# A second buffer for the turned sums of a softmax, and one instead of two for their quarters

## The chip, the cores and the metric

The kernel runs on one core of a Trainium2 chip. The metric is the device time of one execution in microseconds (us), the median of several runs. The profile is of one such execution. The engines are called as the profile has them: PE is the tensor engine (matrix products, into PSUM), DVE is VectorE, ACT is ScalarE, and SP issues the transfers (DMAs).

## What is computed

Two layers of the same kind, one after the other, on `x` of shape (4, 128, 96, 96) in float32. A layer is a block of attention over the pixels of an image, cut here to its lines:

```
g     = maxpool2(conv1x1(x, g_w, g_b))          # 64 channels, 48*48 = 2304 keys
phi   = maxpool2(conv1x1(x, phi_w, phi_b))      # 64 channels, 2304 keys
theta = conv1x1(x, theta_w, theta_b)            # 64 channels, 96*96 = 9216 queries
attn  = softmax(theta^T phi)                    # over the 2304 keys
y     = attn g
x     = W_w y + W_b, normalised by bn_*, + x
```

The divisor of the softmax, one sum of 2304 exponentials for each query, is what the change is about.

## The kernel before

**Tiling.** Keys lie on partitions, queries along the free dimension. The 2304 keys are 18 tiles of 128. The 9216 queries are nine *pairs* of 2 x 512. For one pair and one tile of keys, `scores` (L347) lets PE make a 128 x 1024 tile of products and ACT take its exponential (L357) into one of seven `exp` buffers; `add_up` (L360) lets DVE add that tile to the pair's running `sum` (L366; the first time L364); `values` (L368) lets PE multiply it by `gT` into `av` (L374). After the last tile ACT copies `av` to `halves` (L381): two partial results of 512 columns, which `add_halves` (L453) adds.

**Steps and cycles.** The order of the work on each engine is written out by hand. There are 8 blocks (four images, two layers) of nine pairs, and nine steps of two key tiles to a pair: 648 steps. In step `t`, PE makes the scores of step `t` and then the values of step `t - 1`. Eighteen steps are a *cycle*: its even pair takes s = 0 to 8, its odd pair s = 9 to 17. What else there is to do stands at fixed places s of the cycle:

```
TURNS, HALVES, INVERT = (8, 4), (12, 2), (13, 6)
NORM, PROJECT = (1, 10), (3, 12)
```

The first number is for the even pair, the second for the odd one. A number smaller than the pair's own steps means a place in the next cycle, where the two pairs of the cycle before are called `gone`. So the even pair is turned at s = 8 and 9, inverted at 13, normalised at 1 of the next cycle and projected at 3; the odd pair is turned at 4 and 5 of the next cycle, inverted at 6, normalised at 10 and projected at 12. In the last cycle the even pair's halves and invert come at s = 10 already.

**The divisor.** `sum` has, for each query, 128 partial sums, one on each partition. `turn(h)` (L415) transposes one half of it, 128 x 512, in squares of 32 x 32 into `turned` (L422), and reduces that to 16 columns of `parts` (L423). After both halves, `invert` (L428) transposes the four quarters of `parts` into `four` (L433), reduces them to one sum for each query (L434), takes the reciprocal (L437) and notes the sums for a later check (L438). The reciprocals must then be spread: every query's to all 64 channels. For that two DMAs write them as two rows of 512 into `turned`, whose contents are no longer needed (L443), and two more broadcast each row to 64 partitions of `halves` (L448), which is `rc`. `normalise` (L457) multiplies by it (L458); `multiply` (L460) is the projection on PE (L464), into the two PSUM banks of the tag `misc`; `add` (L469) is DVE's reading of them (L473), with the shift and the residual, back into `x`.

**What else uses the two `misc` banks.** The keys and values of the next block are made in chunks beside the current one, with products on PE (L208, `gphi_ps`) and pooling on DVE (L234). They start at s = 13, 15 and 17 while there are chunks left to make. The next pairs' `theta` (also L208) is made at s = 5.

**Buffers and queues.** The pool `work` has two buffers for a tag where nothing else is said. `turned` has one; `parts`, `sum`, `halves`, `four` and `both` have two. [...] The broadcasts and the stores of the results are issued from the queue of SP.

Of the kernel before, what the change touches and what calls it, by code (L numbers as in the profile page):

```python
# [9 lines left out]
F32 = mybir.dt.float32  # L10
# [6 lines left out]
P = 128  # L17
# [3 lines left out]
QT = 512  # L21
# [22 lines left out]
SQ = 32  # L44
# [9 lines left out]
def shifted_blocks(ctx: ExitStack, tc: tile.TileContext, x: bass.AP, layers, out: bass.AP, flag):  # L54
# [30 lines left out]
    work = ctx.enter_context(tc.tile_pool(name="work", bufs=2))  # L85
# [222 lines left out]
    class Pair:  # L308
# [106 lines left out]
        def turn(self, h):  # L415

            if h == 0:
                self.turned = work.tile(
                    [P, QT], F32, tag="turned", name=f"turned_{self.name}", bufs=1
                )  # L420
                self.parts = work.tile([P, SQ], F32, tag="parts", name=f"parts_{self.name}")
            nc.vector.transpose(self.turned, self.sum[:, ts(h, QT)])  # L422
            nc.vector.tensor_reduce(  # L423
                self.parts[:, ts(h, QT // SQ)],
                self.turned.rearrange("p (b k) -> p b k", k=SQ), AX.X, ALU.add,
            )

        def invert(self):  # L428

            four = work.tile([SQ, P // SQ, SQ], F32, tag="four", name=f"four_{self.name}")  # L430
            both = work.tile([SQ, 2, SQ], F32, tag="both", name=f"both_{self.name}")
            for k in range(P // SQ):
                nc.vector.transpose(four[:, k, :], self.parts[ts(k, SQ), :])  # L433
            nc.vector.tensor_reduce(  # L434
                both[:, 0, :], four.rearrange("p k q -> p q k"), AX.X, ALU.add
            )
            nc.vector.reciprocal(both[:, 1, :], both[:, 0, :])  # L437
            nc.vector.tensor_reduce(notes[:SQ, self.number, :], both, AX.X, ALU.add)  # L438
            self.rc = self.halves[:, QT:]
            n = QT // SQ  # L440
            for h in range(2):
                row = self.turned[h * CI : h * CI + 1, :]
                nc.sync.dma_start(  # L443
                    out=row.rearrange("o (b k) -> o b k", k=SQ), in_=both[ts(h, n), 1, :]
                )
            for h in range(2):
                row = self.turned[h * CI : h * CI + 1, :]
                nc.sync.dma_start(  # L448
                    out=self.rc[ts(h, CI), :],
                    in_=row.unsqueeze(1).to_broadcast([1, CI, QT]),  # L450
                )
# [565 lines left out]
```

## Time and profile before

| what | before |
|---|---|
| median of three runs | 2587.36 us (2585.7 to 2587.54) |
| span of the profiled execution | 2584.3 us |
| DVE: transposes into `turned` (L422) | 142, 705 ns each |
| DVE: reduction of `turned` (L423) | 142, 686 ns each |
| DVE: transposes into `four` (L433) | 284, 199 ns each |
| SP: DMAs of reciprocals into rows of `turned` (L443) | 142, 2 KB each |
| SP: broadcasts from `turned` into `halves` (L448) | 142, 128 KB each |

A group of the profile has its line, engine and operation, its operands as out<-in with their shapes, then how often it ran, and busy time and mean duration. A list of waits has who waited (engine, tile, line), for whom, and then us in all, times and the longest. A timeline has start and length in us; neighbours of one kind are merged, with their number after the x; the bracket at the end has the idle time of the engine before the instruction and what ended it. A matmul's end is modelled and matmuls overlap, so the start of the next one tells more than the length of one. A product of float32 takes two matmul instructions here: one step's scores, two tiles of four products, are 16 of them.

### The profile page before, as it was taken

To read this page: it belongs to the slowest core of one execution; us is meant where nothing else is said; L and a number is where in the kernel's file an instruction comes from. 1 tells how busy PE (TensorE), PEld (TensorE's weight loads), DVE (VectorE), ACT (ScalarE), POOL (GpSimd) and SP (SyncE) were. 2 spreads that over 40 slices of the span, in tenths; PEclk is the share of its full clock that TensorE was granted. 3 is DMA by queue.
4 is the path that set the end of the run, shared out by engine and by line. 5 is a ranking of instruction groups with operands and counts; after the bars stand their busy time and mean duration, and the time that the engine had idled before them with its cause. 6 is when DMAs were issued, how large, how long until landed. Compare 5 with 4: busy or idle time off the path is not lost.

```text
span 2584.3 us, 53389 instructions
## 1 busy us (share of the span) xinstructions
PE 2512.7 (97%) x23058; PEld 1119.8 (43%) x23058; DVE 2122.9 (82%) x2684; ACT 1542.0 (60%) x1511; POOL 0.7 (0%) x6
## 2 busy tenths in 40 slices
PE   9999999999999999999999999999999999999998
PEld 4344434444354443444433444344443354433332
DVE  7888888888888888888888888888888888888887
ACT  5555655556655566555666556555566565666664
POOL 0000000000000000000000000000000000000000
PEclk9999999999999999999999999999999999999999
DMA  4113111111121122222112212211111221122222
GB/s 151 9 6 83 10 10 9 7 8 10 9 18 22 25 26 18 18 18 70 10 10 17 26 22 26 25 10 9 9 7 9 21 23 23 24 26 26 26 26 35
DMA packets 26888, 60.43 MB, mean 23 GB/s; under 512 B 8330, under 2 KB 9236, under 8 KB 26644
## 3 DMA queue, kind: packets, MB, share of 16 engines
q1 hardware_dynamic: 26476, 56.88, 19.5%
q8 instruction: 182, 2.98, 0.5%
q14 instruction: 62, 0.51, 0.1%
q10 hardware_dynamic: 168, 0.07, 0.0%
HBM read 19.14 MB, written 18.87 MB: 15 GB/s over the span
## 4 chain that ended last, share of the span: by engine, by line


## 5 line engine op out<-in xcount | busy, mean ns | idle before, releaser
L357 ACT ACTIVATE exp<-sc,nshift 128x1024 f32<-128x1024 f32 x1296 | 1385.5, 1113 | 959.4 <-PE sc L351 957.9
L366 DVE TENSOR_TENSOR sum<-sum,exp 128x1024 f32<-128x1024 f32 x1151 | 1406.6, 1222 | 204.4 <-ACT exp L357 153.1
L351 PE MATMUL sc<-theta,phi 64*64 64x512 f32 x10368 | 1456.8, 589 | 0.8 <-ACT exp L357 0.8
L374 PE MATMUL av<-exp,gT 64*64 64x512 f32 x10368 | 1400.6, 590 | 0.0
L351 PEld LDWEIGHTS sc<-theta,phi 64*64 64x64 f32 x10368 | 531.5, 133 | 614.3 <-issue 523.0
L374 PEld LDWEIGHTS av<-exp,gT 64*64 64x64 f32 x10368 | 519.4, 133 | 611.0 <-issue 507.0
L422 DVE STREAM_TRANSPOSE turned<-sum 128x512 f32<-128x512 f32 x142 | 100.3, 706 | 174.2 <-DMA halves<-turned 174.2
L208 PE MATMUL gphi_ps<-x,gphiT 64*64 64x512 f32 x1056 | 202.5, 593 | 16.6 <-DVE x L473 16.6
L464 PE MATMUL W_ps<-halves,WT 64*64 64x512 f32 x568 | 84.2, 608 | 44.4 <-DVE halves L458 44.4
L234 DVE TENSOR_REDUCE gphi<-gphi_ps 128x128 f32<-128x512 f32 x144 | 92.3, 680 | 31.8 <-PE gphi_ps L208 24.8
L364 DVE TENSOR_TENSOR sum<-exp,exp 128x1024 f32<-128x1024 f32 x72 | 87.8, 1220 | 19.6 <-ACT exp L357 18.9
L381 ACT COPY halves<-av 128x1024 f32<-128x1024 f32 x71 | 71.9, 1012 | 50.2 <-PE av L374 50.2
L423 DVE TENSOR_REDUCE parts<-turned 128x16 f32<-128x512 f32 x142 | 97.4, 686 | 4.9
L473 DVE SCALAR_TENSOR_TENSOR x<-W_ps,shift,x 128x512 f32<-128x512 f32 x142 | 99.6, 743 | 0.0
L208 PEld LDWEIGHTS gphi_ps<-x,gphiT 64*64 64x64 f32 x1056 | 61.3, 132 | 86.7 <-DVE x L473 45.0
L208 PE MATMUL theta_ps<-x,thetaT 64*64 64x512 f32 x560 | 88.5, 589 | 0.0
L304 DVE STREAM_TRANSPOSE gT<-gphi 32x192 f32<-32x192 f32 x192 | 70.7, 368 | 3.5
L464 PEld LDWEIGHTS W_ps<-halves,WT 64*64 64x64 f32 x568 | 22.1, 133 | 93.3 <-DVE halves L458 75.3
L433 DVE STREAM_TRANSPOSE four<-parts 32x32 f32<-32x32 f32 x284 | 56.4, 199 | 2.9
L455 DVE TENSOR_TENSOR halves<-halves 128x512 f32<-128x512 f32 x71 | 48.5, 683 | 0.0
L458 DVE TENSOR_TENSOR halves<-halves 128x512 f32<-128x512 f32 x71 | 48.5, 683 | 0.0
L208 PEld LDWEIGHTS theta_ps<-x,thetaT 64*64 64x64 f32 x560 | 29.2, 133 | 34.6 <-issue 30.7
(75 smaller groups left out, 217.1 us busy)
## 6 DMA issues: line engine op xcount, KB each, us to landing
halves<-turned SPq DMA_DIRECT2D x142, 128.0 KB
out_dram<-x SPq DMA_DIRECT2D x35, 512.0 KB
x<-in_x_dram SPq DMA_DIRECT2D x18, 768.0 KB
x<-in_x_dram SPq DMA_DIRECT2D x12, 384.0 KB
turned<-both SPq DMA_DIRECT2D x142, 2.0 KB
out_dram<-x SPq DMA_DIRECT2D x4, 128.0 KB
gphi_nat<-in_L_conv_phi_w_dram SPq DMA_DIRECT2D x2, 32.0 KB
rows_other<-in_L_conv_g_b_dram SPq DMA_DIRECT2D x4, 0.2 KB
```

The source lines that it names most:

```text
L208: nc.tensor.matmul(out, lhsT=lhsT, rhs=rhs, start=step == 0, stop=step == 1)
L234: nc.vector.tensor_reduce(self.gphi[:, ts(k, KT)].rearrange("p (h w) -> p h w", w=w), ps.rearrange("p (h a w b) -> p h w a b", a=2, b=2, w=w),
L351: nc.tensor.matmul(ps[ts(c, CI), ts(h, QT)], lhsT=self.blk.phi[ts(h, CI), ts(2 * k + c, CI)], rhs=self.th[ts(h, CI), :], start=True, stop= ...
L357: nc.scalar.activation(e, ps, AF.Exp, bias=nshift)
L364: nc.vector.tensor_add(self.sum, self.es[0], e)
L366: nc.vector.tensor_add(self.sum, self.sum, e)
L374: nc.tensor.matmul(self.av[ts(h, CI), ts(r, QT)], lhsT=self.blk.gT[ts(r, CI), k, :], rhs=e[ts(r, CI), ts(h, QT)], start=(k == 0), stop=(k ...
L381: nc.scalar.copy(self.halves, self.av)
L422: nc.vector.transpose(self.turned, self.sum[:, ts(h, QT)])
L423: nc.vector.tensor_reduce(self.parts[:, ts(h, QT // SQ)], self.turned.rearrange("p (b k) -> p b k", k=SQ), AX.X, ALU.add,)
L464: nc.tensor.matmul(self.pss[h][ts(c, CI), :], lhsT=self.blk.w.W[ts(h, CI), ts(c, CI)], rhs=self.y[ts(h, CI), :], start=True, stop=True,)
L473: nc.vector.scalar_tensor_tensor(dst, self.pss[h], self.blk.w.shift, dst, op0=ALU.add, op1=ALU.add)
```

## The change

The tile `turned` gets two buffers, like the other tags of its pool. The rows in which a pair's reciprocals stand while they are spread are then not the ones that the next pair's sums are turned into. In turn `four` gets one buffer instead of two. In a partition's bytes `turned` takes 2048 more, and `four` 512 less.

```diff
             if h == 0:
                 self.turned = work.tile(
-                    [P, QT], F32, tag="turned", name=f"turned_{self.name}", bufs=1
+                    [P, QT], F32, tag="turned", name=f"turned_{self.name}"
                 )
                 self.parts = work.tile([P, SQ], F32, tag="parts", name=f"parts_{self.name}")
...
         def invert(self):
 
-            four = work.tile([SQ, P // SQ, SQ], F32, tag="four", name=f"four_{self.name}")
+            four = work.tile(
+                [SQ, P // SQ, SQ], F32, tag="four", name=f"four_{self.name}", bufs=1
+            )
             both = work.tile([SQ, 2, SQ], F32, tag="both", name=f"both_{self.name}")
```

Nothing else is changed.

## The prediction, made before the change was run

> **What bounds the kernel now.** The page comes first: which engine is full, and in every slice or only in some.
>
> ```profile
> PE 2512.7 (97%) x23058; PEld 1119.8 (43%) x23058; DVE 2122.9 (82%) x2684; ACT 1542.0 (60%) x1511; POOL 0.7 (0%) x6
> ```
>
> PE is the engine to relieve or to keep fed; VectorE at 82% and ScalarE at 60% have room. The page gives no chain (its part 4 is empty), so the path has to be found from the waits. The list of waits, cut to VectorE and to PE (us in all, times, longest us):
>
> ```profile
> DVE turned L422 <- DMA halves<-turned: 174.2, 35, 5.7
> PE W_ps L464 <- DVE halves L458: 44.4, 35, 5.3
> PE gphi_ps L208 <- DVE x L473: 16.6, 21, 0.8
> ```
>
> VectorE's longest wait is the one the change is aimed at: 35 times about 5 us. That alone is no gain, since VectorE has slack. The other two lines count: PE stands still for the projection (35 times, waiting for the normalise on L458) and for the next keys' chunk (21 times, waiting for the add on L473). 35 is also the number of cycles that have a previous odd pair. The timeline of VectorE in one cycle joins them (start us, length us, what; in brackets the idle time and its releaser):
>
> ```profile
> 1199.45 2.56 DVE L366 TENSOR_TENSOR sum<-sum,exp 128x1024 f32<-128x1024 f32 x2 [0.88 <-ACT exp L357]
> 1206.85 0.71 DVE L422 STREAM_TRANSPOSE turned<-sum 128x512 f32<-128x512 f32 x1 [4.85 <-DMA halves<-turned]
> ...
> 1213.13 0.68 DVE L458 TENSOR_TENSOR halves<-halves 128x512 f32<-128x512 f32 x1
> 1213.73 3.88 DVE L366 TENSOR_TENSOR sum<-sum,exp 128x1024 f32<-128x1024 f32 x3
> 1217.53 1.40 DVE L473 SCALAR_TENSOR_TENSOR x<-W_ps,shift,x 128x512 f32<-128x512 f32 x2
> ```
>
> The transpose of the even pair (s = 8) may not overwrite `turned` until the odd pair's broadcast out of its rows (issued at s = 6) has landed, at 1206.85. Everything VectorE has queued behind it is late, among it the normalise (s = 10) and the add (s = 12). Now PE in the same stretch:
>
> ```profile
> 1208.86 2.26 PE L374 MATMUL av<-exp,gT 64*64 64x512 f32 x16
> 1210.57 2.26 PE L351 MATMUL sc<-theta,phi 64*64 64x512 f32 x16
> 1213.87 1.09 PE L464 MATMUL W_ps<-halves,WT 64*64 64x512 f32 x8 [1.03 <-DVE halves L458]
> 1214.78 1.90 PE L374 MATMUL av<-exp,gT 64*64 64x512 f32 x16
> 1216.49 1.04 PE L351 MATMUL sc<-theta,phi 64*64 64x512 f32 x8
> 1218.33 1.31 PE L208 MATMUL gphi_ps<-x,gphiT 64*64 64x512 f32 x5 [0.79 <-DVE x L473]
> ```
>
> Read the starts, not the lengths. 16 matmuls take 1.72 us from start to start (1208.86 to 1210.57), so 8 take 0.86; a plain step of 32 takes 3.43 us and one with 8 more 4.29. Step 12 should be 4.29; from its first scores (1210.57) to the next step's (1216.49) it is 5.92, a loss of 1.63. The bracket says only 1.03, because a matmul counts as busy to its modelled end, past the point where its successor could have started. In step 13 the chunk was due 0.86 after 1216.49, at 1217.35, and started at 1218.33: 0.98 lost.
>
> I subtracted these nominal lengths from all 648 steps. Sixteen of the eighteen places in the cycle lose nothing or next to it (6.2 us in all at s = 1, where the values wait for ScalarE's copy of `av`). Step 12 loses 62.7 us in 35 cycles, 7.85 of them in the last; step 13 loses 21.5 us in 21 cycles. Why the last is so large:
>
> ```profile
> 2547.46 1.99 PE L464 MATMUL W_ps<-halves,WT 64*64 64x512 f32 x8 [5.31 <-DVE halves L458]
> 2549.22 3.34 PE L374 MATMUL av<-exp,gT 64*64 64x512 f32 x16
> 2552.39 1.89 PE L351 MATMUL sc<-theta,phi 64*64 64x512 f32 x16
> ```
>
> There the even pair's invert also stands ahead of the normalise at s = 10. PE idles 5.31 us, then needs 1.76 us for 8 matmuls and 3.17 for 16, twice the usual.
>
> [...] the idle times of about 1 us have no such sequel. [...] the sums of s = 9 and 10, whose exponentials were there, were done only after the transpose. [...] 97% hides 84 us, and the repeated hole of 4.85 us is a buffer's release.
>
> **The change, part by part.**
>
> *Second `turned`.* Pairs alternate, so even pairs have one buffer and odd pairs the other. The even transpose at s = 8 now needs the even pair's broadcast issued at s = 13 of the cycle before (thirteen steps, some 50 us earlier), and that pair's normalise, which waited for this landing, has run on VectorE at s = 1. The odd transpose at s = 4 likewise. The 174.2 us of waiting go. The landing is still needed by the odd pair's own normalise, so I place that again in the cycle shown, without the stall:
> - Transpose and reduce of the even pair from 1202.0 to 1203.4.
> - s = 9: its exponentials end near 1203.9; one sum (1.21) and the second turn (1.4), to 1206.4.
> - s = 10: its exponentials end at 1206.3 and 1207.4 (ScalarE starts them at 1205.22); two sums to 1208.8, the normalise to 1209.5.
> - The broadcast landed at 1206.85, 1.9 us before VectorE asks. PE wants the product at 1210.57 + 1.72 = 1212.28, 2.8 us after it is there. No wait is left.
>
> *The chunk at s = 13.* With no lag, the add at s = 12 is like that at s = 3, where no stall precedes: the scores start at 1177.10 and the adds run from 1180.85 to 1182.25, that is +3.75 to +5.15 us. The chunk is due at +4.29 + 0.86 = +5.15. Its first bank is free at +4.45, its second just in time. In the cycle shown the second bank was 1.58 us late against its due time and the loss was 0.98, so half a microsecond of lateness costs nothing. I take 0 and keep 0.1 us x 21 = 2 us for the range.
>
> *Last cycle.* From the transpose's start to the normalise's end are 2538.08 to 2547.40 = 9.3 us without a pause. Begun 5.65 earlier, the normalise ends at 2541.75; PE is due at 2540.25 + 1.72 = 2541.97. So it just fits, and the half clock is not entered: 7.85 us come back, or 7 if the margin of 0.2 is missed.
>
> *One `four`.* Its transposes overwrite what the reduce on L434 read nine steps and more earlier, on the same engine, whose order already gives that: nothing. The DMAs, their sizes and their order on the SP queue are the same. The normalise may need a wait of its own for the broadcast: the trace has 36 such events of 21 ns at L458 for the even pairs, so 35 x 0.02 = 0.7 us more on VectorE, in its slack.
>
> *Sum.* 62.7 + 21.5 = 84.2 us less, and some 1 us kept back for the chunk and the last cycle: 2587.36 - 83 = 2504.
>
> **The rivals.**
> - *Only the idle time of the page comes back*, or something is left of the wait at s = 12 and 13: 44.4 + 16.6 = 61.0, so 2526. For it: these are the only numbers that the profile calls waits. Against it: the starts of the matmuls, which show the steps longer by 84.
> - *The wait moves.* The normalise inherits the DMA wait and PE still waits: no change, 2587. It would take a landing 4.7 us later (1211.6 instead of 1206.85) before PE waits at all, and some 7 us later to lose what is lost now. The chain from the invert's end to the landing took 10.8 to 11.0 us in all 35 cycles.
> - *PE without its pauses is granted less clock*, slower: one half-rate window of 6.8 us (as at 2545) in each of 35 cycles would cost 3.4 x 35 = 119 us, 2504 + 119 = 2623. Against it: PE already runs some 60 us per cycle without a pause at full clock, and the only half-rate windows of the trace, apart from start and end, follow the idle time.
>
> **How the numbers follow.** Full gain 0.86, at 2504; part of it 0.08, at 2526; wait moves 0.03, at 2587; slower 0.03, at 2623. The predicted time is the first. A bottom of 2500 allows for 84 us, all of the hitches, and the spread of 1.8 us among the runs of before; the top of 2516 takes in 2 us at the chunk, 1 in the last cycle and 0.2 us left in each of 35 steps 12. Faster 0.94, same 0.03, slower 0.03.
>
> **What would show it.** Right: the wait of `turned` for the broadcast and both PE waits gone from the lists; VectorE's busy time the same at about 2123 us and its share up; step 12 at 4.29 us; the second sum before L422 and L422 itself back to back; no half clock before the end. Wrong: L458 with a DMA as its releaser, L208 still waiting for L473, PE starts wider than 0.86 us per 8 in plain steps, or more ScalarE or PE waits for exponentials' buffers.

## The result, and the profile after

| | before | after |
|---|---|---|
| median | 2586.82 us (2585.7 to 2587.54) | 2496.19 us (2495.89 to 2496.32) |
| span of the profiled execution | 2584.3 us | 2493.8 us |

The median of before is now of four runs, one more than ahead. The ratio is 0.965, with a 95% interval of 0.9633 to 0.9667: 90.6 us less, where 83 were forecast. The direction and the main mechanism held; the time lies 4 us below the range. In the changed kernel lines behind L430 are two higher: L458, L464 and L473 are now L460, L466 and L475.

The first part of the page after, busy time by engine:

```profile
PE 2483.7 (100%) x23058; PEld 897.7 (36%) x23058; DVE 2133.0 (86%) x2684; ACT 1541.7 (62%) x1511; POOL 0.7 (0%) x6
```

The same number of instructions on each engine as before, and PE has no pause left that the page can see. The list of waits after, for PE alone, is complete with four lines, all of them from the start or the end:

```profile
PE warm_ps L565 <- POOL ident masks.py:199: 1.4, 1, 1.4
PE sc L351 <- ACT exp L357: 0.8, 1, 0.8
PE gphi_ps L244 <- DVE thetaT L121: 0.6, 1, 0.6
PE W_ps L496 <- DVE halves L489: 0.5, 1, 0.5
```

The 44.4 us for the normalise and the 16.6 for the add are gone. VectorE's wait for the broadcast (174.2 us) is gone from its list as well; what it waits for now is ScalarE's exponentials. The timeline of VectorE after, in the cycle that answers to the one shown of before:

```profile
1159.67 2.55 DVE L366 TENSOR_TENSOR sum<-sum,exp 128x1024 f32<-128x1024 f32 x2 [0.88 <-ACT exp L357]
1162.25 0.71 DVE L422 STREAM_TRANSPOSE turned<-sum 128x512 f32<-128x512 f32 x1
...
1169.06 0.69 DVE L460 TENSOR_TENSOR halves<-halves 128x512 f32<-128x512 f32 x1
...
1174.54 1.40 DVE L475 SCALAR_TENSOR_TENSOR x<-W_ps,shift,x 128x512 f32<-128x512 f32 x2
```

Sum and transpose stand back to back. The normalise comes 6.8 us after the transpose begins and waits for nothing; before, the hole of 4.85 us stood ahead of both. The timeline of PE after, steps 12 and 13:

```profile
1171.14 1.90 PE L351 MATMUL sc<-theta,phi 64*64 64x512 f32 x16
1172.86 1.04 PE L466 MATMUL W_ps<-halves,WT 64*64 64x512 f32 x8
1173.72 1.90 PE L374 MATMUL av<-exp,gT 64*64 64x512 f32 x16
1175.44 1.04 PE L351 MATMUL sc<-theta,phi 64*64 64x512 f32 x8
1176.30 1.04 PE L208 MATMUL gphi_ps<-x,gphiT 64*64 64x512 f32 x8
```

Step 12 is 1171.14 to 1175.44, 4.30 us, its nominal length; the chunk starts 0.86 after that, as it should. Summed over all 648 steps, what goes beyond the nominal lengths is 90.2 us less than before, and what is left lies nearly all in the first cycle.

So 90.2 us came back. The prediction counted 62.7 at step 12 and 21.5 at step 13, and left 6.2 us at s = 1 where they were. All but 0.2 of those came back too.

### The profile page after: what moved, and what is told of

It reads as the page before. It is cut to its first block, busy times and chain, and to the rows that moved or that the text cites. A ratio compares the mean times of both kernels' runs of the same rounds, so it can differ in the third digit from the quotient of the medians.

```text
span 2493.8 us, 53372 instructions
## 1 busy us (share of the span) xinstructions
PE 2483.7 (100%) x23058; PEld 897.7 (36%) x23058; DVE 2133.0 (86%) x2684; ACT 1541.7 (62%) x1511; POOL 0.7 (0%) x6
## 4 chain that ended last, share of the span: by engine, by line
## 5 line engine op out<-in xcount | busy, mean ns | idle before, releaser
L351 PE MATMUL sc<-theta,phi 64*64 64x512 f32 x10368 | 1248.6, 589 | 0.8 <-ACT exp L357 0.8
L374 PE MATMUL av<-exp,gT 64*64 64x512 f32 x10368 | 1229.6, 589 | 0.0
L374 PEld LDWEIGHTS av<-exp,gT 64*64 64x64 f32 x10368 | 398.8, 133 | 713.3 <-issue 691.8
L351 PEld LDWEIGHTS sc<-theta,phi 64*64 64x64 f32 x10368 | 398.4, 133 | 713.1 <-issue 687.9
L208 PE MATMUL gphi_ps<-x,gphiT 64*64 64x512 f32 x1056 | 137.3, 589 | 0.0
L422 DVE STREAM_TRANSPOSE turned<-sum 128x512 f32<-128x512 f32 x142 | 100.2, 706 | 1.2
L475 DVE SCALAR_TENSOR_TENSOR x<-W_ps,shift,x 128x512 f32<-128x512 f32 x142 | 99.6, 744 | 0.0
L466 PE MATMUL W_ps<-halves,WT 64*64 64x512 f32 x568 | 73.7, 589 | 0.0
L304 DVE STREAM_TRANSPOSE gT<-gphi 32x192 f32<-32x192 f32 x192 | 70.6, 368 | 3.5
L208 PE MATMUL theta_ps<-x,thetaT 64*64 64x512 f32 x560 | 72.8, 589 | 0.0
L208 PEld LDWEIGHTS gphi_ps<-x,gphiT 64*64 64x64 f32 x1056 | 45.2, 132 | 68.2 <-issue 59.2
L460 DVE TENSOR_TENSOR halves<-halves 128x512 f32<-128x512 f32 x71 | 48.6, 685 | 0.0
L466 PEld LDWEIGHTS W_ps<-halves,WT 64*64 64x64 f32 x568 | 21.7, 133 | 39.3 <-issue 38.7
L208 PEld LDWEIGHTS theta_ps<-x,thetaT 64*64 64x64 f32 x560 | 21.7, 133 | 38.4 <-issue 29.0
```

Source lines behind the costliest of these rows:

```text
L208: nc.tensor.matmul(out, lhsT=lhsT, rhs=rhs, start=step == 0, stop=step == 1)
L351: nc.tensor.matmul(ps[ts(c, CI), ts(h, QT)], lhsT=self.blk.phi[ts(h, CI), ts(2 * k + c, CI)], rhs=self.th[ts(h, CI), :], start=True, stop= ...
L374: nc.tensor.matmul(self.av[ts(h, CI), ts(r, QT)], lhsT=self.blk.gT[ts(r, CI), k, :], rhs=e[ts(r, CI), ts(h, QT)], start=(k == 0), stop=(k ...
L466: nc.tensor.matmul(self.pss[h][ts(c, CI), :], lhsT=self.blk.w.W[ts(h, CI), ts(c, CI)], rhs=self.y[ts(h, CI), :], start=True, stop=True,)
L475: nc.vector.scalar_tensor_tensor(dst, self.pss[h], self.blk.w.shift, dst, op0=ALU.add, op1=ALU.add)
```

## The experiments

Every kernel was run beside the one before on the same chip. Times are medians. "Loss" is again a step's length beyond the nominal one, from the first matmul of its scores to the first of the next step's, where nothing else is said.

### Which half of the change it is

`four_alone`: before, with this alone:

```diff
-            four = work.tile([SQ, P // SQ, SQ], F32, tag="four", name=f"four_{self.name}")
+            four = work.tile(
+                [SQ, P // SQ, SQ], F32, tag="four", name=f"four_{self.name}", bufs=1
+            )
```

> Only the second half of the change: one buffer for `four`, and still one for `turned`. My theory (the gain is the release of `turned` alone): 2587 us, within 0.2% of before, with the wait of L422 for the broadcast still at about 174 us. Rival (the smaller footprint or the other placement of the tiles matters): a part of the 90 us is gained, below 2580.

2586.14 us, ratio 0.9999 (0.999 to 1.0007). VectorE still waits 174.4 us at L422. One buffer for `four` costs nothing and brings nothing; in the change it gives back 512 of the 2048 bytes of a partition that the second `turned` takes.

### The reuse distance, not the number of buffers

`turned_early`: before, with one buffer, but the odd pair's turn and invert two steps earlier:

```diff
-TURNS, HALVES, INVERT = (8, 4), (12, 2), (13, 6)
+TURNS, HALVES, INVERT = (8, 2), (12, 2), (13, 4)
```

> One buffer for `turned` as before, but the odd pair is turned at s = 2 and 3 and inverted at s = 4 instead of 4, 5 and 6, so that its broadcast lands two steps (6.9 us) earlier, near 1200 in the cycle shown, before VectorE comes to the even transpose at 1202. My theory (what costs is the distance between the broadcast and the next use of the rows, not the number of buffers): 2496 to 2500 us. Rival (two buffers are needed, or VectorE is overloaded at s = 2 to 4 and PE waits at s = 5): above 2520.

2495.97 us, ratio 0.965 (0.9635 to 0.9665): the time of the change, without its memory. The timeline of VectorE in `turned_early`, from the end of the odd pair's invert to the even transpose:

```profile
1150.33 0.21 DVE L438 TENSOR_REDUCE notes<-both 32x2 f32<-32x64 f32 x1
...
1160.06 2.56 DVE L366 TENSOR_TENSOR sum<-sum,exp 128x1024 f32<-128x1024 f32 x2 [0.88 <-ACT exp L357]
1162.65 0.71 DVE L422 STREAM_TRANSPOSE turned<-sum 128x512 f32<-128x512 f32 x1
```

12.1 us lie between the invert's end and the transpose. The chain needs 10.8 to 11.0, so nothing waits.

### The last cycle and the half clock

`last_own`: one buffer for all pairs but the last even one, which gets a tile of its own (with one `four`):

```diff
-                    [P, QT], F32, tag="turned", name=f"turned_{self.name}", bufs=1
+                    [P, QT], F32, tag="turned_last" if self.number == late else "turned",
+                    name=f"turned_{self.name}", bufs=1
```

> The last cycle's even pair alone gets a tile of its own for `turned`; all other pairs share one as before. My theory (the wait of 5.31 us there also halves the clock of PE afterwards): step 12 of the last cycle gives back 7.85 us, so 2586.8 - 7.9 = 2579, and the window of half clock near 2545 us is gone. Rival (only the idle time counts): 2586.8 - 5.3 = 2581.5. No effect: 2587.

2578.43 us, 7.9 us less than before (2586.34), ratio 0.997 (0.9959 to 0.9982). The timeline of PE in `last_own` at that place:

```profile
2541.25 1.04 PE L467 MATMUL W_ps<-halves,WT 64*64 64x512 f32 x8
2542.11 1.90 PE L374 MATMUL av<-exp,gT 64*64 64x512 f32 x16
2543.82 1.90 PE L351 MATMUL sc<-theta,phi 64*64 64x512 f32 x16
```

8 matmuls in 0.86 us and 16 in 1.71, where before had 1.76 and 3.17 and the windows view gives it a granted clock of 0.50 from 2547 to 2552 us. So the idle time (5.31) and the slow matmuls after it (2.4) both belong to this one wait. Losses in all other cycles stay as they were.

### What a wait on VectorE costs, moved elsewhere

`norm_at_8`: the changed kernel with the odd pair's normalise two steps earlier, right behind the even transpose:

```diff
-NORM, PROJECT = (1, 10), (3, 12)
+NORM, PROJECT = (1, 8), (3, 12)
```

> The changed kernel (two buffers), but the odd pair's normalise stands at s = 8, behind the even transpose, instead of s = 10. It then waits for the broadcast itself, about 3.4 us on VectorE (from about 1203.4 to 1206.85 in the cycle shown of before). My theory (a wait of VectorE costs only where PE stands behind what is queued): no loss at the projection, since the normalise is done earlier than PE asks, but the add at s = 12 is late and the chunk's second bank with it by about 1.7 us, in 21 cycles: 36 us, so 2532 us. Rival (the wait costs the same wherever it stands on VectorE): near 2587. Rival (VectorE makes it up before s = 12): 2496.

2538.62 us, ratio 0.9815 (0.9799 to 0.9831). The timelines of VectorE and of PE in `norm_at_8`:

```profile
1187.48 0.69 DVE L460 TENSOR_TENSOR halves<-halves 128x512 f32<-128x512 f32 x1 [3.32 <-DMA halves<-turned]
...
1197.03 1.40 DVE L475 SCALAR_TENSOR_TENSOR x<-W_ps,shift,x 128x512 f32<-128x512 f32 x2
```

```profile
1192.98 1.40 PE L466 MATMUL W_ps<-halves,WT 64*64 64x512 f32 x8
1193.84 2.26 PE L374 MATMUL av<-exp,gT 64*64 64x512 f32 x16
1195.56 1.40 PE L351 MATMUL sc<-theta,phi 64*64 64x512 f32 x8
1197.83 1.31 PE L208 MATMUL gphi_ps<-x,gphiT 64*64 64x512 f32 x5 [0.86 <-DVE x L475]
```

The hole of 3.32 us is back on VectorE, yet the projection waits for nothing; the chunk does, since the add is still late. Losses are 32.1 us at s = 13 and 6.2 at s = 1 in the chunks' cycles, and 3.7 in the last cycle, which I had not expected: VectorE has no pause there in which to catch up, and PE waits 2.44 us for the last normalise. The rival of 2587 falls: the same kind of wait cost 90 us in one place of the queue and 42 in another.

### What the late bank costs

The chunk waits for two banks, one freed by each of the two adds. The next three kernels are the changed one with dead additions of about 0.6 us on VectorE at s = 12, in the 21 cycles with a chunk at s = 13; `(0, 3)` puts three between the two adds, `(3, 0)` three ahead of both, `(0, 1)` one between:

```diff
+                for _ in range(fill[h]):
+                    nc.vector.tensor_add(self.rc, self.rc, self.rc)
                 dst = self.blk.xt[:, ts(2 * self.p + h, QT)]
...
+            if s == PROJECT[1] and t + 1 in keys:
+                take = lambda pair=pair: pair.add((0, 3))
```

`fill_between`, (0, 3):

> The changed kernel with three dead additions of 128x512 on VectorE (about 0.6 us each, 1.8 in all) between the two adds at s = 12, in the 21 cycles with a chunk at s = 13 alone. Only the second of the two banks comes late: it is free 0.36 us before PE asks now, so 1.45 us after. My theory (three of four sub-arrays wait for the second bank, and its lateness is paid in full): 21 x 1.45 = 30, so 2526 us. Rival (as in my prediction: half a microsecond of the second bank's lateness is free, and the first bank decides): 2496 to 2515.

`fill_ahead`, (3, 0):

> The same three dead additions, ahead of both adds at s = 12. Both banks come 1.8 us later: the first one 0.75 us after PE asks, the second one 1.45. My theory (the second bank alone sets the loss): the same 2526 us as with the additions between the two, though one sub-array now is less far ahead. Rival (the first bank decides): 21 x 0.8 = 17 us, 2513, and more than with the additions between.

2533.92 us and 2534.17 us (ratios 0.9797 and 0.9799, intervals of 0.0016 to each side). They are alike, as the theory had it, and so the first bank's lateness is not what counts; but both lose 1.8 us in each of the 21 cycles, not 1.45. The timeline of VectorE in `fill_between` shows the reason: three dead additions move the second add not by 1.8 us, but by 2.05 (1194.79 to 1196.84).

```profile
1194.79 2.13 DVE L475 TENSOR_TENSOR halves<-halves 128x512 f32<-128x512 f32 x3
1196.84 0.74 DVE L477 SCALAR_TENSOR_TENSOR x<-W_ps,shift,x 128x512 f32<-128x512 f32 x1
```

Where the loss is found differs. By the first matmul of a step, `fill_between` loses 27.4 us at s = 13 and 10.0 at the places s = 14, 15 and 1; `fill_ahead` loses 31.2 at s = 13 and 6.0 at s = 1. The timeline of PE in `fill_between` shows why:

```profile
1195.53 1.02 PE L208 MATMUL gphi_ps<-x,gphiT 64*64 64x512 f32 x2
1197.63 0.65 PE L208 MATMUL gphi_ps<-x,gphiT 64*64 64x512 f32 x3 [1.09 <-DVE x L477]
```

One product, of two instructions, starts in time, at 1195.53; its bank is free. The three others start 2.1 us later, 0.05 after the end of the second add; one of them writes the free bank too, but stands in the program behind one that waits. The timelines give these matmuls as 64*64, and four run beside each other: 16 take 1.72 us, while one follows the other on one of the four parts every 0.43 (1195.26 and 1195.69 in `fill_one`, below). One of the four is now ahead of the others. The first matmul of a step is then the one of the part in front.

A second measure leaves that part out: from the eighth matmul of a step's scores, in order of their starts, to the eighth of the next step's. The eighth is always one of a part that is behind. By it, `fill_between` and `fill_ahead` lose 37.4 us each at s = 13, and nothing at the other places.

`fill_one`, (0, 1):

> The changed kernel with one dead addition (0.6 us) between the two adds at s = 12 of the 21 cycles with a chunk, instead of three. With three, the loss was 37.8 us in 21 cycles, 1.8 each, which is the whole length of the three. My theory (the second bank comes just in time, and its lateness is paid in full): 21 x 0.6 = 12.6, so 2508.8 us. Rival (as predicted: half a microsecond of lateness is free): 2496 to 2499.

2503.22 us, 7.0 us above the changed kernel: 0.33 a cycle, between the two expectations. Mine had left out that the second bank is free early in the changed kernel. There the chunk starts 0.35 us after the second add's end, and 0.05 after it where it waits, so 0.30 us are spare. The one addition moves the second add by 0.60 us and the three move it by 2.05; that makes 0.30 and 1.75 us a cycle, where 0.33 and 1.78 were measured. So what goes beyond the spare time is paid in full. The timeline of PE in `fill_one`, long after the chunk:

```profile
1195.26 0.59 PE L374 MATMUL av<-exp,gT 64*64 64x512 f32 x1
1195.54 0.60 PE L351 MATMUL sc<-theta,phi 64*64 64x512 f32 x3
1195.69 1.74 PE L374 MATMUL av<-exp,gT 64*64 64x512 f32 x12
```

Starts come as one and three. The one is already in the values (L374) 0.28 us before the three start their last scores (L351), and one instruction takes 0.43, so the lead is 0.71 us; it stays so step after step up to s = 1. In this kernel step 13 loses nothing by its first matmul, and the 0.3 us of each cycle is found at s = 1; by the eighth, all 7.0 us are at s = 13.

### The chunk moved away

`chunk_moved`: before, with the chunk of s = 13 begun at s = 1:

```diff
-KEYS = (15, 17, 31)
+KEYS = (15, 17, 19)
```

> Before, with one buffer for `turned`, but the keys' chunk that began at s = 13 begins at s = 1 of the same cycle's end (KEYS 15, 17, 19 instead of 15, 17, 31), so that no chunk stands right behind the projection. My theory (the chunk's wait for the second bank puts one sub-array of PE up to 0.66 us ahead of the three others; the loss of 0.28 us at s = 1 and a part of the loss at s = 12 are that lead being closed again): losses at s = 13 and s = 1 vanish, and step 12 loses only what it loses today after a cycle without such a chunk, about 1.3 us, so 34 x 1.3 + 7.9 = 52 and 2496 + 52 = 2548 us. Rival (what I predicted: step 12 loses 62.7 us by itself, and the 6.2 us at s = 1 belong to ScalarE's copy): 2496 + 62.7 = 2559, or 2565 with the 6.2 us.

2638.08 us, ratio 1.0201 (1.0185 to 1.0216): a miss, because the edit moved more than the chunk. The transposes into `gT` (L304) that follow a third chunk came along to s = 3 to 6, ahead of the invert, and made the broadcast late: in the cycle shown it lands at 1233.23, 1.4 us before the scores of step 12, where it was 3.7 us in the kernel before. The timeline of PE in `chunk_moved`:

```profile
1234.64 1.90 PE L351 MATMUL sc<-theta,phi 64*64 64x512 f32 x16
1240.26 1.91 PE L464 MATMUL W_ps<-halves,WT 64*64 64x512 f32 x8 [3.73 <-DVE halves L458]
1241.93 2.83 PE L374 MATMUL av<-exp,gT 64*64 64x512 f32 x16
1244.59 1.90 PE L351 MATMUL sc<-theta,phi 64*64 64x512 f32 x16
```

Over the whole run PE waits 91.2 us for the normalise, where it was 44.4 before, and the mean granted clock is 0.981, where it was 0.998. In the cycle shown, after a wait of 3.73 us, 8 matmuls take 1.67 us and 16 take 2.66, and the windows view has the granted clock at 0.50 from 1240.4 to 1243.8. For the question asked the run tells nothing.

`chunk_only` keeps those transposes where they were:

```diff
-KEYS = (15, 17, 31)
+KEYS = (15, 17, 19)
...
-                spreads[t + 2] = (blocks[n], j // len(KEYS))
+                spreads[t + 14] = (blocks[n], j // len(KEYS))
```

> Before, with one buffer for `turned` and the chunk at s = 1 instead of s = 13 once more, but the transposes into `gT` that follow a third chunk (L304) stay at s = 15 to 18, where they were. In chunk_moved they came along to s = 3 to 6 and pushed the invert at s = 6, and so the broadcast, some 3 us later. My theory (the wait for the second bank makes the losses at s = 13 and s = 1 and the part of step 12 that goes beyond 1.3 us): 2548 us, up to 2556 if the pooling now at s = 2 still delays the invert by a few tenths. Rival (step 12 loses 62.7 us by itself, the 6.2 us at s = 1 belong to ScalarE's copy): 2559 to 2565.

2557.89 us, ratio 0.9888 (0.9872 to 0.9903), 29.1 us less than before (2586.99). The losses at s = 13 and at s = 1 are gone, 21.5 and 6.0, though ScalarE's copy stands at s = 1 as it did. So the 6.0 belong to the chunk. The other half of my theory seems to fall: step 12 still loses 62.0 us (62.7 before), not 52. But this kernel makes a lead of its own, at the chunk of s = 17. Three lines from the timelines of PEld (PE's weight loads) and PE in `chunk_only`:

```profile
1148.22 0.14 PEld L208 LDWEIGHTS gphi_ps<-x,gphiT 64*64 64x64 f32 x3 [0.24 <-DVE gphi L234]
1148.70 0.59 PE L351 MATMUL sc<-theta,phi 64*64 64x512 f32 x1
1148.71 0.59 PE L208 MATMUL gphi_ps<-x,gphiT 64*64 64x512 f32 x2
```

Three products wait for VectorE's pooling of the chunk before, and the fourth part is in the scores while they are still in the chunk. By the eighth matmul, 14 cycles lose 0.42 us each at s = 17, 6.0 us with one smaller loss, and step 12 loses 56.6 us, where the kernel before loses 54.8. So step 12 has the same loss of its own in both kernels, near the 52 of my theory, and the rest of the 62 is a lead that ends there. `chunk_only` missed its 2548 because 6.0 us were lost anew at s = 17, and because step 12 by itself costs some 3 to 5 us more than I had put in.

## Why the prediction was right, and where it failed

**Right.** *Second `turned`*: the 174.2 us went, and nothing took their place. The placement by hand had the normalise ending 2.8 us before PE asks; after, it ends at 1169.75 and the projection starts at 1172.86, 3.1 us later. *Last cycle*: the 7.85 us came back whole (`last_own`, 7.9). *One `four`*: nothing (`four_alone`). *Reading starts, not waits*: the page's waits, 61.0 us, would have been too small by 30. The rivals "the wait moves" (whose "some 7 us later" is 6.4 by its own numbers, 4.7 and the 1.63 lost in that cycle) and "less clock" did not come about; the windows view has the granted clock at 1.00 up to 2490 us.

**The step that failed** is the sentence on sixteen of eighteen places, with its term of 6.2 us "at s = 1, where the values wait for ScalarE's copy". I took a wait that stands beside a loss for its cause and kept it out of the sum. Had it gone in, and had I not kept back 1 us, the sum would have been 84.2 + 6.0 = 90.2 (the other 0.2 belong to the first cycle), against 90.6 measured. Of the 7.8 us between 2504 and 2496.19, 6.0 are this term, 0.8 are what was kept back, and 0.5 are the shift of the median before. The timeline of PE before, around s = 1, shows what I overlooked:

```profile
1240.26 2.11 PE L351 MATMUL sc<-theta,phi 64*64 64x512 f32 x14
1241.79 0.64 PE L374 MATMUL av<-exp,gT 64*64 64x512 f32 x1
1241.79 0.59 PE L351 MATMUL sc<-theta,phi 64*64 64x512 f32 x1
1242.21 1.89 PE L374 MATMUL av<-exp,gT 64*64 64x512 f32 x15
```

One product of the values starts at 1241.79, beside the last of the scores, and its fellows at 1242.21: one part of PE is ahead. In this cycle the late add had let one product of the chunk start at 1218.33 and the three others 0.66 us later. My measure took the first matmul of each step, and that is the part that is ahead. It was charged 1.02 us at s = 13; the other three were held for 1.02 + 0.66. The part in front lost 0.28 more at s = 1, where it alone had to wait for the copy to free `av`, and the other 0.38 at the next step 12, where all four had to wait. So the 0.28 us were the chunk's stall, booked six steps too late and under the name of the instruction that stopped the part in front. The eighth matmul shows it for the whole kernel before: 35.0 us are lost at s = 13 (1.67 in each of 21 cycles), not 21.5; 54.8 at step 12, not 62.7; and nothing at s = 1. So the two terms of the sum were mis-sized as well, the one at step 12 by 7.9 us too much and the one at step 13 by 13.5 too little; what the two lack together, 5.6 us, is nearly all of the term left out. The list of waits agrees: waits of weight loads for the copy are 20.6 us in 71 pairs before and 21.1 after, while the loss at s = 1 went from 6.2 us to nothing. A wait that is as long in the kernel without the loss isn't its cause.

The traces show in which order matmuls start around such a wait. While the three products wait in `fill_between`, the free part does not run on: nothing starts between its product's second instruction (1195.95) and 1197.63. After the wait in the run before, the starts are not in the order of the program: at 1219.23 us a matmul of the second scores starts on the part in front, ahead of three matmuls of the chunk (1219.46) that stand before it in the program.

**A second weak step** did no harm, by luck: that half a microsecond of the second bank's lateness costs nothing. It was read off one cycle, by the first matmul again. By the eighth, the bank 1.58 us late against its due time cost 1.67 us, which leaves nothing free, and `fill_one` agrees. The prediction had the second bank free just in time; in the changed kernel the adds end at 1175.94, 0.36 before the chunk asks, so nothing was to be paid.

**The range** was built from what could go wrong in the terms I had. Its bottom, 2500, assumed that no loss outside the two steps could come back.

## What to carry to other kernels

A hole on an engine with slack is worth what stands behind it in that engine's queue and is awaited by the engine that is full: the same broadcast cost 90 us where the transpose waited for it, 42 where the normalise waited right behind the transpose, and nothing where the normalise came two steps later. Where a buffer's release is late, look at the order before paying for a second buffer; `turned_early` had the same time with one. When four parts of PE run beside each other, take the lateness of the parts behind, not the first matmul of a step, and follow a lead until it is closed: here 0.28 us of a stall in each of 21 cycles was booked six steps after it happened.

## What the runs showed of the hardware that was not expected

One part of PE was ahead of the other three: by 0.66 us up to s = 1 and by 0.38 from there to the next step 12 in the run before, by 0.71 in `fill_one`. It stayed ahead until all four waited together, in the run before at step 12. While the three waited for a bank in `fill_between`, the part in front made the two instructions of its own product and then stood still too, so the hold-up of 1.8 us left a lead of 0.84 (the second instruction of the second scores starts at 1198.13 on that part and at 1198.97 on the others).

Around two long waits the windows view has PE's granted clock at one half. In the run before it is 0.50 for 6.8 us from 2545.3 on, which is still within the wait of 5.31 us (up to 2547.46); it is 1.00 from 6 us up to there, and the 34 other waits for the normalise are 1.0 to 1.6 us long. In `chunk_moved` it is 0.50 from 1240.4 to 1243.8, after the wait of 3.73. After one of 2.44 us in `norm_at_8`, 8 matmuls took 0.91 us, which is not half the speed. How long a wait has to be, these runs do not show. By the starts the two long waits are 5.49 and 3.90 us, 0.2 longer, as a matmul counts as busy to its modelled end.
